# A selective-scan convolution with a gated FFN: another queue for one load, fewer idle products at the start, and the last group's products in another order

## The chip, the cores and the metric

The kernel runs on one core of a Trainium2 chip. Five engines work side by side, each through its own list of instructions: TensorE (PE, with its weight loads as PEld), VectorE (DVE), ScalarE (ACT), GpSimd (POOL) and SyncE (SP), which here only issues transfers. Semaphores order them. The metric is the device time of one execution in microseconds (us); lower is better.

## The reference, cut to what matters

```
# cond: a long convolution per head, K from the state space's poles
dtA = (-exp(log_A_real) + 1j*A_imag) * exp(log_dt)[:, None]
Ct  = (C[...,0] + 1j*C[...,1]) * (exp(dtA) - 1) / A
K   = 2 * einsum('hn,hnl->hl', Ct, exp(dtA[:,:,None] * arange(512))).real     # 32 heads x 512
y   = causal_conv(x, K) + x * D[:, None]                                      # 128 x 32 x 512
y   = y * (arange(512) < itok[:, None])[:, None, :]
# ffn along the length, each input rounded to fp8 (e4m3) with its scale
g = fp8(y) @ gate_w.T ; u = fp8(y) @ up_w.T                                   # 512 -> 1376
h = silu(g * scale) * (u * scale)
out = x + (fp8(h) @ down_w.T) * scale                                         # 1376 -> 512
```

There are 128 sequences (the batch), 32 heads and a length of 512. The FFN runs along the length, so that each pair of batch and head is one row of it, 4096 rows in all.

## The kernel before, in words

The length lies on the partitions in four chunks of 128, and a group is four heads times 128 sequences, 512 columns, so there are eight groups (g = 0 to 7).

**K and the convolution.** K is made on the chip in three batches of heads: heads 0 to 3, 4 to 15 and 16 to 31 (`batches`, L155). For a batch, `Powers` computes angles, magnitudes, sines and coefficients on VectorE and ScalarE, and `response` (L337) multiplies them on PE into `kp`, copies that to `kt` on VectorE and writes it to DRAM (`kpad`, L346). For a head, `toeplitz` (L435) reads 128 shifted rows of `kpad` back with two DMAs (L441, L442), which gives a Toeplitz matrix `st`. PE convolves with it in fp32 (`convolve` for the first two batches, `convolve8` with fewer products for the third, with `sp` and `cp` as accumulators). `conv` (L553) adds the shared part on VectorE, rounds to fp8 (`q`, L558) and masks it (L568).

**The first 30 us.** SyncE issues the loads in program order: the state space's planes `sm`, the scales (a broadcast of 3 KB), the lengths (a broadcast of 64 KB), group 0's input (1 MB, L121), and six of the eleven chunks of the gate matrix (1.5 MB, L146). Then come K's write and the Toeplitz reads of the first heads. ScalarE's first work is a table load, `sa` (L218) and the square `a2` (L220); then it waits for the step sizes. [...]`keep_busy` (L231) puts products of a zero tile (`nothing`) into its list: 14, then 12 behind `wim`, then 8 behind `th` (L356), then K's products of the first batch, then 22 more (L374).

**A group.** `gate_up` (L593) makes the 11 chunks of the hidden layer. For each, four products of `gw` into `gp` and four of `uw` into `up`; ScalarE takes silu (L612), VectorE multiplies (L613) into `v`, and two chunks at a time are rounded to fp8's grid by ScalarE (L586) and three VectorE operations (L589 to L591) into `hq`. Chunks 9 and 10 are rounded one by one, last. The batches of chunks are 0, 1-2, 3-4, 5-6, 7-8, 9, 10.

`Down` then multiplies `hq` by the down matrix, one tile `dp` of 128 rows of the length at a time, 11 products each (`multiply`, L644); `put_out` (L658) adds the result to `x` on VectorE (L662) and issues the output's DMA. While VectorE is still rounding, PE convolves the first two heads of the next group and starts tiles 0 and 1 without the two last chunks (`LATE` = 9, L634). Then it alternates: head 2, the rest of tile 0, head 3, the rest of tile 1, and at last tiles 2 and 3. Most groups have two accumulators for four `dp` tiles, so that tile 2 begins when tile 0 has been put out. In group 6 PE does only five products of tile 2 (`SOME`, L751) before the last gate/up; the other six and tile 3 follow behind it. Group 7's last tile is done in two halves of 256 columns.

**The order.** Each engine works through its list in order. The lists come from a planner that places instructions by its own estimate of when they are ready, within the order that `after(...)` prescribes. An accumulator or buffer is taken from a pool by its tag and is free when its last reader is done.

**The end.** `verdict` (L530) collects checks of the numbers on VectorE; one product `bp` (L542) sums them over partitions; the flag `any_bad` is read by every engine (L857), which then branches over a second, wider version of the kernel (L858).

Of the kernel before, what the change touches and what calls it, by code (L numbers as in the profile page):

```python
# [57 lines left out]
def ssm_fp8_ffn(  # L58
# [11 lines left out]
    nc = tc.nc  # L70
# [4 lines left out]
    IC = (I + P - 1) // P  # L75
    IP = IC * P
    NA, NB = 16, 32
    HG = 4
# [53 lines left out]
    gw = const.tile([P, LC, IP], F32, name="gw")  # L132
# [4 lines left out]
    def load_gate_up(w, src, i0, i1, queue=nc.sync):  # L137
        return queue.dma_start(w[:, :, i0:i1], src[:, i0:i1].rearrange("(c p) i -> p c i", p=P))
# [4 lines left out]
            nc.sync.dma_start(dw[0 : I - FI * P, FI, :], downT[FI * P :, :])  # L143

    IH = 6 * P
    load_gate_up(gw, gateT, 0, IH)  # L146

# [4 lines left out]
    batches = [(0, HG), (HG, HB), (HB, H)]  # L155
# [4 lines left out]
    EIGHT = len(batches) - 1  # L160
# [43 lines left out]
    def after(done):  # L204

        return tc.issue_after(done.ins)
# [11 lines left out]
    signs_there = nc.scalar.activation(sa, ca, AF.Copy, scale=sign)  # L218
    with after(signs_there):
        square_there = nc.scalar.activation(a2, aim, AF.Square)  # L220
    nc.gpsimd.tensor_mul(U, cb, aim)
    parts_there = nc.gpsimd.tensor_mul(V, sa, aim)
    ex = small("ex", [P, 2, H])
# [7 lines left out]
    def keep_busy(n, there=None):  # L231

        nothing = ps.tile([P, 512], F32, name="nothing", tag="gp")
        if there is not None:
            nc.tensor.matmul(nothing[0:NA, 0:NB], idx[:, 0:NA], there, start=True, stop=True)
        for _ in range(n):
            nc.tensor.matmul(nothing, still[:, 0:P], still, start=True, stop=True)  # L237
# [113 lines left out]
    th = small("th")  # L351
    with after(exp_there), after(square_there):
        silu_there = first.magnitudes()
    with after(silu_there):
        first_sines = first.sines(lambda: nc.scalar.activation(th, wre, AF.Tanh, scale=0.5))
    keep_busy(8, th)  # L356


    with after(parts_there):
# [12 lines left out]
    done, copied, _ = first.response()  # L372
# [38 lines left out]
    with after(build_mask(mask, all_bits, range(1))):  # L411
# [4 lines left out]
        done = build_mask(mask, all_bits, range(1, LC))  # L416
# [53 lines left out]
    def convolve(h, st, xg, xs, j, scale, pool, before=None, bufs=2):  # L470

        if h >= batches[EIGHT][0]:
            return convolve8(st, xg, xs, j, scale, pool, before, bufs)
        b = slice(j * B, (j + 1) * B)
        k3, k2, K2, K1, K0 = (st[:, n, :] for n in range(1, 6))
        sp = ps.tile([P, B], F32, name="sp", tag="gp")  # L480
        nc.tensor.matmul(sp, K2, xs[:, 0, b], start=True, stop=True)  # L481
        t = shared[j]
        with after(before) if before else ExitStack():
            copied = nc.scalar.activation(t[:, 1, :], sp, AF.Copy, scale=scale)
        cp = ps.tile([P, LC, B], F32, name="cp")
        nc.tensor.matmul(cp, K0, xg[:, :, b], start=True, stop=False)  # L486

        nc.tensor.matmul(cp[:, 2:4, :], K1, xg[:, 0:2, b], start=False, stop=False)  # L488
        nc.tensor.matmul(cp[:, 1, :], k2, xg[:, 2, b], start=False, stop=False)
        done = nc.tensor.matmul(cp[:, 3, :], k3, xg[:, 0, b], start=False, stop=True)  # L490
        return cp, twice(t[:, 0:2, :]), done, copied
# [53 lines left out]
    def narrow():  # L545
        with ExitStack() as arm:
# [3 lines left out]
            vp = arm.enter_context(tc.tile_pool(name="vp", bufs=3))  # L550
            gm, um, dm = (w.bitcast(BF16)[:, :, 1::2] for w in (gw, uw, dw))

            def conv(g, q, j, xg, xs, before, behind=None):  # L553

                st, loaded = toeplitz(stp, g * HG + j)
                cp, t, convolved, copied = convolve(g * HG + j, st, xg, xs, j, inv[:, 0:1], vp, before)
                with after(behind) if behind else ExitStack():
                    nc.vector.scalar_tensor_tensor(  # L558
                        pairs(q[:, :, j * B : (j + 1) * B]),
                        pairs(cp),  # L560
                        inv[:, 0:1],
                        t,
                        ALU.mult,
                        ALU.add,
                        saturate=False,
                    )
                words = q.bitcast(I32)[:, :, j * B // 4 : (j + 1) * B // 4]
                made = nc.vector.tensor_tensor(words, words, mask.bitcast(I32), ALU.bitwise_and)  # L568
                if j == HG - 1:
                    for n in range(2):  # L570
                        junk = vp.tile([P, T], F32, name="s")
                        nc.scalar.activation(  # L572
                            junk.bitcast(BF16),
                            q[:, n * LC // 2 : (n + 1) * LC // 2, :].rearrange("p c t -> p (c t)"),
                            AF.Abs,
                            accum_out=fin[:, 2 * g + n : 2 * g + n + 1],
                        )
                return convolved, made, loaded, copied
# [55 lines left out]
            LATE = IC - 2  # L634
# [45 lines left out]
            xg, xs = x0, xs0  # L680
# [23 lines left out]
            for g in range(G):  # L704
                sum_next = []
                hq, multiplied, sums, quantised = gate_up(
                    g, q, (lambda: sum_next.append(add_chunks(x_next, 1))) if g == 0 else lambda: None
                )
                if g == 2:
                    others[1].response()  # L710
                if g == G - 1:
                    break
                some = {0: (others[1].angles(), 2), 1: (itertools.chain(others[1].coefficients(), others[1].products()), 5)}
                tags = ["dp", "dp", "dp", "cp" if g == G - 2 else "dp"]
                d = Down(g, hq, xg, whole, tags, *some.get(g, ()))
                xg = x_next
                xs = sum_next.pop() if sum_next else xs
                q = yp.tile([P, LC, T], F8, name="q")

                def head(j, before):  # L720
                    return conv(g + 1, q, j, xg, xs, before)

                with after(multiplied):
                    head(0, sums[-2])
                    done, made, loaded, _ = head(1, sums[-1])
                if g == 0:
                    with after(loaded):
                        load_down()  # L730
                with after(sums[-1]):
                    if g == 0:
                        silu_there = others[1].magnitudes()
                    else:
                        list(itertools.islice(lows, 4))
                with after(done):
                    d.multiply(0, 0, LATE)
                    done = d.multiply(1, 0, LATE)
                for n in range(2):
                    with after(done):  # L740
                        done, made, loaded, _ = head(2 + n, sums[-1])
                    with after(done):
                        done = d.multiply(n, LATE, IC)
                    with after(made):
                        added = d.put_out(n)
                if g + 2 < G:
                    with after(loaded):
                        x_next = load_x(g + 2)
                        if (g + 2) * HG >= batches[EIGHT][0]:
                            xs = load_sums(g + 2)  # L750
                SOME = IC // 2  # L751
                with after(done):
                    done = d.multiply(2, 0, SOME)
                if g == G - 2:
                    continue
                with after(done):
                    done = d.multiply(2, SOME, IC)
                with after(added):
                    added = d.put_out(2)
                with after(done):  # L760
                    d.multiply(3, 0, IC)
                with after(added):
                    added = d.put_out(3)
                if g == 0:
                    with after(silu_there):
                        others[1].sines()
                if (g + 2) * HG < batches[EIGHT][0]:
                    with after(added):
                        xs = add_chunks(x_next, 1)

            with after(multiplied):
                d.multiply(2, SOME, IC)
                done = d.multiply(3, 0, IC)
            with after(quantised):
                d.put_out(2)
                added = d.put_out(3)
            d = Down(g, hq, xg, halves, ["dp", "gp", "up", "gp", "up"])
            with after(done):
                d.multiply(0, 0, LATE)
                done = d.multiply(1, 0, LATE)  # L780
            for n in range(len(halves)):
                with after(done):
                    done = d.multiply(n, LATE if n < 2 else 0, IC)
                    if n == len(halves) - 2:
                        with after(added):
                            verdict(done)
                d.put_out(n)
# [118 lines left out]
```

## Time and profile before

| | |
|---|---|
| median of 3 runs | 319.92 us (319.6 to 320.04) |
| the profiled execution's own time | 320.19 us |
| its span, first to last instruction | 318.4 us |
| PE busy | 308.7 us, 97% of the span |
| VectorE busy | 267.6 us, 84% |
| ScalarE busy | 182.4 us, 57% |
| GpSimd busy | 26.2 us, 8% |
| mean granted TensorE clock | 0.997 |
| DMA | 43.77 MB, 137 GB/s in the mean |

The profiled execution's time holds the span and some 1.8 us around it. Busy is what the profile's records cover; a matmul's record is longer than the time after which the next one may start, so that busy PE can hide small gaps, which show in the distance of starts only. In the timeline a row is the start, the time to the end of the last of its instructions, the engine, the line and operation, the tile written and those read, and the number of instructions. In the chain of work that ended last, a row is start, length and what it was.

### The profile page before, as it was taken

To read this page: it belongs to the slowest core of one execution; us is meant where nothing else is said; L and a number is where in the kernel's file an instruction comes from. 1 tells how busy PE (TensorE), PEld (TensorE's weight loads), DVE (VectorE), ACT (ScalarE), POOL (GpSimd) and SP (SyncE) were. 2 spreads that over 40 slices of the span, in tenths; PEclk is the share of its full clock that TensorE was granted. 3 is DMA by queue.
4 is the path that set the end of the run, shared out by engine and by line. 5 is a ranking of instruction groups with operands and counts; after the bars stand their busy time and mean duration, and the time that the engine had idled before them with its cause. 6 is when DMAs were issued, how large, how long until landed. Compare 5 with 4: busy or idle time off the path is not lost.

```text
span 318.4 us, 4632 instructions
## 1 busy us (share of the span) xinstructions
PE 308.7 (97%) x1583; PEld 165.4 (52%) x1583; DVE 267.6 (84%) x480; ACT 182.4 (57%) x372; POOL 26.2 (8%) x66
## 2 busy tenths in 40 slices
PE   8989999999999999999999999999999999999992
PEld 3455446544554446644576446644576446644441
DVE  5874999799989999648997699958997699969991
ACT  5825758567673668356673567456664576267600
POOL 5720000000000000120002200120001200000000
PEclk9999999999999999999999999999999999999998
DMA  3699999442036400698036921498046900010022
GB/s 95 260 234 382 264 357 309 129 134 89 12 86 193 141 1 2 132 312 228 1 99 194 280 90 48 110 286 219 2 99 171 256 4 2 1 66 3 0 106 102
DMA packets 32722, 43.77 MB, mean 137 GB/s; under 512 B 3539, under 2 KB 18899, under 8 KB 32691
## 3 DMA queue, kind: packets, MB, share of 16 engines
q1 hardware_dynamic: 29075, 34.61, 35.1%
q0 software_dynamic: 2560, 6.29, 9.2%
q10 hardware_dynamic: 1056, 2.49, 2.1%
q8 instruction: 14, 0.23, 0.3%
q14 instruction: 17, 0.14, 0.1%
HBM read 34.84 MB, written 8.55 MB: 136 GB/s over the span
## 4 chain that ended last, share of the span: by engine, by line
PE 78%; DVE 11%; ACT 3%; DMA 2%; issue 2%; POOL 1%; DVEq 0%; POOLq 0%; ACTq 0%
PE gp L604 22%; PE up L604 21%; PE dp L649 20%; PE cp L486 3%; PE sp L455 3%; PE cp L467 3%; DVE v L589 2%; DVE hq L590 2%; PE cp L465 2%; DVE v L613 2%; DVE q L558 2%; PE cp L488 2%; ACT mag L273 1%; PE sp L481 1%; DMA st<-kpad 1%
## 5 line engine op out<-in xcount | busy, mean ns | idle before, releaser
L604 PE MATMUL gp<-q,gw 128*128 128x512 fp8e4 x352 | 90.5, 379 | 0.7 <-DVE q L568 0.7
L604 PE MATMUL up<-q,uw 128*128 128x512 fp8e4 x352 | 90.3, 379 | 0.5 <-DVE v L613 0.5
L612 ACT ACTIVATE s<-gp,psc 128x512 f32<-128x512 f32 x88 | 59.9, 681 | 48.2 <-PE gp L604 48.1
L649 PE MATMUL dp<-hq,dw 128*128 128x512 bf16 (+1 forms) x363 | 80.6, 372 | 0.2
L613 DVE SCALAR_TENSOR_TENSOR v<-up,psc,s 128x512 f32<-128x512 f32 x88 | 65.4, 744 | 13.8 <-PE up L604 9.0
L589 DVE SCALAR_TENSOR_TENSOR v<-m,v 128x1024 f32<-128x1024 bf16 (+1 forms) x56 | 55.3, 988 | 5.4 <-ACT m L586 4.5
L586 ACT ACTIVATE m<-v 128x1024 bf16<-128x1024 f32 (+1 forms) x56 | 48.8, 872 | 17.4 <-DVE v L613 16.8
L604 PEld LDWEIGHTS <-uw 128*128 128x128 bf16 x352 | 34.5, 98 | 42.2 <-issue 0.8
L604 PEld LDWEIGHTS <-gw 128*128 128x128 bf16 x352 | 34.3, 98 | 42.4 <-issue 1.0
L590 DVE SCALAR_TENSOR_TENSOR hq<-m,v 128x1024 bf16<-128x1024 bf16 (+1 forms) x56 | 55.1, 984 | 0.1
L649 PEld LDWEIGHTS <-dw 128*128 128x128 bf16 x363 | 35.4, 98 | 37.1 <-issue 1.8
L662 DVE SCALAR_TENSOR_TENSOR xg<-dp,nsc,xg 128x512 f32<-128x512 f32 (+1 forms) x33 | 23.9, 731 | 10.8 <-PE dp L649 10.8
L558 DVE SCALAR_TENSOR_TENSOR q<-cp,inv,shared 128x512 fp8e4<-128x512 f32 x32 | 23.8, 745 | 9.6 <-PE cp L490 7.0
L572 ACT ACTIVATE s<-q 128x1024 bf16<-128x1024 fp8e4 x16 | 16.8, 1048 | 20.9 <-DVE q L568 20.9
L591 DVE TENSOR_SCALAR hq<-hq 128x1024 bf16<-128x1024 bf16 (+1 forms) x56 | 20.1, 358 | 0.2
L113 POOL DMA_DIRECT2D xs<-xT x4 | 3.2, 809 | 197.5 <-DVE q L558 114.6
L459 ACT ACTIVATE sh<-sp,inv 128x384 f32<-128x384 f32 x16 | 9.1, 571 | 15.9 <-PE sp L455 15.9
L237 PE MATMUL nothing<-still 128*128 128x512 bf16 x56 | 15.1, 430 | 1.4 <-POOL still L174 1.4
L486 PE MATMUL cp<-xg,st 128*128 128x512 f32 x32 | 16.4, 594 | 0.0
L455 PEld LDWEIGHTS sp<-xs,st 128*128 128x128 f32 x96 | 12.9, 192 | 1.7
L467 PEld LDWEIGHTS cp<-xg,st 128*128 128x128 f32 x96 | 13.2, 191 | 0.8
L455 PE MATMUL sp<-xs,st 128*128 128x128 f32 x96 | 13.3, 275 | 0.0
(143 smaller groups left out, 240.7 us busy)
## 6 DMA issues: line engine op xcount, KB each, us to landing
st<-kpad SPq DMA_DIRECT2D x48, 192.0 KB, 3.7
xg<-xT SPq DMA_DIRECT2D x8, 1024.0 KB, 6.6
outT<-xg SPq DMA_DIRECT2D x31, 256.0 KB, 4.7
xs<-xT POOLq DMA_DIRECT2D x8, 512.0 KB, 6.8
dw<-downT SPq DMA_DIRECT2D x1, 2560.0 KB, 13.3
st<-kpad SPq DMA_DIRECT2D x16, 128.0 KB, 4.3
xs<-xT POOLq DMA_DIRECT2D x8, 256.0 KB, 5.4
gw<-gateT SPq DMA_DIRECT2D x1, 1536.0 KB, 12.1
```

Of the source, the lines that this page charges most:

```text
L455: nc.tensor.matmul(sp[:, n, :], k, xs[:, n, b], start=True, stop=True)
L467: done = nc.tensor.matmul(cp[:, AT[c], :], k, xg[:, AT[x], b], start=c != 3, stop=True)
L486: nc.tensor.matmul(cp, K0, xg[:, :, b], start=True, stop=False)
L558: nc.vector.scalar_tensor_tensor(pairs(q[:, :, j * B : (j + 1) * B]), pairs(cp), inv[:, 0:1], t, ALU.mult, ALU.add, saturate=False,)
L586: done = nc.scalar.activation(m[:, 0:F], v, AF.Abs, scale=2.0**20 * (1.0 + 2.0**-6), accum_out=acc)
L589: nc.vector.scalar_tensor_tensor(v, m[:, 0:F], 1.5 * 2.0**14, v, ALU.max, ALU.add)
L590: nc.vector.scalar_tensor_tensor(out, m[:, 0:F], 1.5 * 2.0**14, v, ALU.max, ALU.subtract)
L604: multiplied = nc.tensor.matmul(o, w[:, c, i * P : (i + 1) * P], q[:, AT[c], :], start=(c == 0), stop=(c == LC - 1),)
L612: nc.scalar.activation(s, gp, AF.Silu, scale=pgate)
L613: product = nc.vector.scalar_tensor_tensor(v[:, (i - i0) * T : (i - i0 + 1) * T], up, pup, s, ALU.mult, ALU.mult)
L649: done = nc.tensor.matmul(self.dps[n], dm[:, i, c * P : (c + 1) * P], self.hq[:, i, t0:t1], start=(i == 0), stop=(i == IC - 1),)
L662: added = nc.vector.scalar_tensor_tensor(o, self.dps[n], ndown, o, ALU.mult, ALU.add)
```

## The change

Four edits.

1. The load of the first six gate chunks leaves SyncE's list, where it stood behind the input's load, and goes to ScalarE's, behind the square.
2. Eight zero products in front of the first batch's K become four.
3. In groups whose next group belongs to the third batch of heads (g = 3 to 6), the rest of tile 0 and its `put_out` come ahead of the VectorE operation that rounds head 2's convolution to `q`. PE's order stays.
4. Group 6 does all of tile 2, with its output, before the last gate/up. Group 7 starts three tiles without the last two chunks instead of two.

```diff
     IH = 6 * P
-    load_gate_up(gw, gateT, 0, IH)
...
     with after(signs_there):
         square_there = nc.scalar.activation(a2, aim, AF.Square)
+
+    with after(square_there):
+        load_gate_up(gw, gateT, 0, IH, nc.scalar)
...
-    keep_busy(8, th)
+    keep_busy(4, th)
...
-            def conv(g, q, j, xg, xs, before, behind=None):
+            def conv(g, q, j, xg, xs, before, behind=None, between=None):
                 st, loaded = toeplitz(stp, g * HG + j)
                 cp, t, convolved, copied = convolve(g * HG + j, st, xg, xs, j, inv[:, 0:1], vp, before)
+                if between:
+                    behind = between(convolved)
...
+                def finish(n, done):
+                    with after(done):
+                        return d.multiply(n, LATE, IC)
...
-                for n in range(2):
-                    with after(done):
-                        done, made, loaded, _ = head(2 + n, sums[-1])
-                    with after(done):
-                        done = d.multiply(n, LATE, IC)
-                    with after(made):
-                        added = d.put_out(n)
+                if (g + 1) * HG < batches[EIGHT][0]:
+                    for n in range(2):
+                        with after(done):
+                            done, made, loaded, _ = head(2 + n, sums[-1])
+                        done = finish(n, done)
+                        with after(made):
+                            added = d.put_out(n)
+                else:
+                    ends = []
+                    def first_out(convolved):
+                        ends.append(finish(0, convolved))
+                        return d.put_out(0)
+                    with after(done):
+                        head(2, sums[-1], first_out)
+                    with after(ends[0]):
+                        done, made, loaded, _ = head(3, sums[-1])
+                    done = finish(1, done)
+                    with after(made):
+                        added = d.put_out(1)
...
-                SOME = IC // 2
                 with after(done):
-                    done = d.multiply(2, 0, SOME)
+                    done = d.multiply(2, 0, IC)
+                with after(added):
+                    added = d.put_out(2)
                 if g == G - 2:
                     continue
-                with after(done):
-                    done = d.multiply(2, SOME, IC)
-                with after(added):
-                    added = d.put_out(2)
...
             with after(multiplied):
-                d.multiply(2, SOME, IC)
                 done = d.multiply(3, 0, IC)
             with after(quantised):
-                d.put_out(2)
                 added = d.put_out(3)
             d = Down(g, hq, xg, halves, ["dp", "gp", "up", "gp", "up"])
-            with after(done):
-                d.multiply(0, 0, LATE)
-                done = d.multiply(1, 0, LATE)
+            for n in range(3):
+                with after(done):
+                    done = d.multiply(n, 0, LATE)
             for n in range(len(halves)):
                 with after(done):
-                    done = d.multiply(n, LATE if n < 2 else 0, IC)
+                    done = d.multiply(n, LATE if n < 3 else 0, IC)
```

More of the change, by code (lines that the diff above doesn't have):

```diff
@@ L718, in narrow, with head @@
                 q = yp.tile([P, LC, T], F8, name="q")
-                def head(j, before):
-                    return conv(g + 1, q, j, xg, xs, before)
+                def head(j, before, between=None):
+                    return conv(g + 1, q, j, xg, xs, before, between=between)
+                def finish(n, done):
+                    with after(done):
+                        return d.multiply(n, LATE, IC)
                 with after(multiplied):
```

## The prediction

> **What bounds the kernel now.** The page comes first: PE is busy 97% of the span and the chain that ended last is 78% PE, so time comes only from stretches where PE has nothing useful to do: the start, two spots per group, and what follows the last matmul. The chain in order of time gives the start:
>
> ```profile
> 10.70 0.23 DVE ga L330
> ...
> 12.67 2.22 DMA kpad<-kt
> 14.89 0.02 issue
> 14.90 3.05 DMA st<-kpad
> 17.95 0.14 issue
> 18.09 0.46 PE sp L481 x2
> ```
>
> K goes out to DRAM and comes back as Toeplitz tiles before the first convolution at 18.09. The timeline shows what stands before it:
>
> ```profile
> 2.61 0.51 SPq L138 DMA_DIRECT2D gw<-gateT  x1
> ...
> 9.84 1.90 PE L237 MATMUL nothing<-still 128*128 128x512 bf16 x8
> ...
> 11.67 0.44 PE L341 MATMUL kp<-ang,ga 128*32 128x32 f32 x8
> ```
>
> `ga` is ready at 10.70 + 0.23 = 10.93, but K's matmuls start at 11.67, behind eight zero products. And K's write, issued at 12.67, follows gate's load on SyncE's queue. By windows of 1 us (last two columns: share of the DMA engines, GB/s):
>
> ```profile
> 11.00:12.00 1.00, 1.00 (x12) 0.46 (x10) 0.42 (x6) 1.00 (x6) 0.67 (x1) 1.00 0.99 399
> 12.00:13.00 1.00, 1.00 (x10) 0.54 (x7) 0.70 (x2) 1.00 (x6) 0.94 (x4) 1.00 0.54 214
> 13.00:14.00 1.00, 1.00 (x7) 0.46 (x5) 0.97 (x3) 0.98 (x2) 0.90 (x2) 1.00 0.54 191
> 14.00:15.00 1.00, 1.00 (x6) 0.42 (x5) 0.96 (x2) 0.70 (x2) 1.00 (x2) 1.00 0.05 12
> ```
>
> About half of the engines carry gate until 14; K's 18 KB land at 14.89, just after. Then the timeline of the groups whose next heads are of the third batch (g = 3 to 6), here g = 6:
>
> ```profile
> 277.39 0.75 DVE L662 SCALAR_TENSOR_TENSOR xg<-dp,nsc,xg 128x512 f32<-128x512 f32 x1
> 277.56 1.88 PE L649 MATMUL dp<-hq,dw 128*128 128x512 bf16 x7
> ...
> 279.94 1.02 PE L604 MATMUL gp<-q,gw 128*128 128x512 fp8e4 x4 [0.50 <-DVE q L568]
> ```
>
> Undisturbed down products start every 0.2157 us (four take 0.86 in the chain) and the last one shows 0.38; seven would take 6 x 0.2157 + 0.38 = 1.67, not 1.88. The missing 0.20 is tile 2 waiting for the accumulator that the first output frees at 278.14. Afterwards PE waits for the fourth head's q. At the end:
>
> ```profile
> 298.93 12.15 PE L649 MATMUL dp<-hq,dw 128*128 128x512 bf16 x61
> ...
> 303.30 0.42 DVE L591 TENSOR_SCALAR hq<-hq 128x1024 bf16<-128x1024 bf16 x1
> ```
>
> PE runs without a gap, but chunks 7 and 8 of hq come only at 303.72. Behind the last matmul stands SyncE (by line: duration min/median/max, first and last start; then its queue's waits):
>
> ```profile
> L857 SPq TENSOR_LOAD <-any_bad x1: 488/488/488, 312.0 to 312.0; - x1
> L665 SPq DMA_DIRECT2D outT<-xg x7: 332/332/333, 306.7 to 313.1; - x7
> L858 SPq COMPARE_BRANCH  x1: 45/45/45, 313.4 to 313.4; - x1
> L858 SPq EVENT_SEMAPHORE  x8: 17/17/17, 316.2 to 316.7; - x8
> SPq L858 <- SPq L858: 2.7, 1, 2.7
> ```
>
> SyncE reads the flag at 312.0, issues the last output at 313.1, branches at 313.4, comes to life 2.7 us later, and its row of semaphore waits runs to the end at 318.4.
>
> **What the skill says.** "TensorE: Matmul & The Clock Gate", on why a gap is 56 ns and not 53.3, gives 215.7 ns from start to start for 512 columns on a warm array; this trace has 0.86/4 = 0.2157, the price used below. The same page, on the clock gate, lets PE cool after some 3.4 us of idling; here PE idles 0.95 us before the first convolution and stays at clock 1.00. "DMA: Bandwidth & Descriptors", Queues, rings and completion order: each issuing engine has its own ring on every DMA engine, a ring is drained in order, and rings take turns. The windows above agree with the first half (K's write ends with gate's load); two full rings side by side are not shown by any run yet. The same page, Issuing engines are not separate DMA queues: another queue adds no bandwidth. So the total of input (1 MB) and gate (1.5 MB) takes as long as before once it runs.
>
> **The change, part by part.**
>
> *Four zero products fewer.* 4 x 0.2157 = 0.86 would let K start at 10.81; `ga` at 10.93 plus some 0.05 (as q to gp, 27.36 to 27.41) holds it to 10.98. Gain 0.69. VectorE's small work ends at 11.45, before it must copy K (12.30 - 0.69 = 11.61). The 22 products that follow cover PE as before.
>
> *Gate's first load on ScalarE's queue.* ScalarE issues it at 3.32, after the square; two such issues took 0.42 and 0.71 there, and ScalarE then waits 2.4 us for its exponentials in any case: cost nothing, 0.4 to 0.7 without that cover. On SyncE it passes nothing that waits. The transfer: at 3-5 us the engines are 3 to 4% busy (2 and 13 GB/s), the input, as I read it, stuck behind the two small broadcasts on its ring. I expect gate to fill this from about 4.3 (some 1 us from issue to data: after the read issued at 14.90 the engines are at 0.04 until 16 and at 0.68 from then) and both, 2.5 MB at some 400 GB/s = 6.3 us, to be in by about 11 on all engines. The input then lands later than its 2.14 + 8.7 = 10.84, near 11.5, still ahead of the add of its chunks (12.51 - 0.6). The lengths, landing at 8, have 2.1 us of GpSimd's wait before the masks as cover. K's write then finds empty rings. The third batch's write, 88 KB alone on the engines, took about 2.0 from issue to reading back (SyncE's three waits on such writes are 9.9 with one of 6.4 and the first 1.8, plus 0.33 to issue); with a fifth of the rows about 1.58. Against 2.22 this is a gain of 0.64; bounds: none, if gate is still running, and 0.8. SyncE's later issues all follow K's landing, and DMA is nearly full from 16 to 55 us on work that starts with it, so all of it shifts along. Start: -1.33; PE's 22 products cap the start's gain at 18.09 - 16.45 = 1.64.
>
> *First output ahead of the third head's q.* As built, VectorE's order in g = 3 to 6 is: shared part, output 0, q of head 2, shared part of head 3, mask, q of head 3. The same work, with the mask no longer waiting directly behind its q. Output 0's product is complete at 275.95, when VectorE is still on the shared part, so nothing waits. Output 0 then ends near 277.0, and tile 2 starts without waiting: by the same reading (four in 1.16, 1.22, 1.23 where 1.03 is due, seven in 1.88) 0.13 + 0.19 + 0.20 + 0.20 = 0.72. Tile 3 needs output 1, at g = 5 ready 0.1 before its turn and now some 0.3 earlier: no new wait.
>
> *Tile 2 of g = 6 whole before the last gate/up; three tiles without two chunks.* PE's work is unchanged: six down products move from behind the last gate/up to before it. They hide the wait for q: before, 7 x 0.2157 + 0.20 after 277.56 is 279.27, and gp starts at 279.94: 0.67 gone. Now gp starts at 277.56 + 13 x 0.2157 = 280.37. But at the other end these six covered VectorE. hq 7 and 8 are ready 303.72 - 279.94 = 23.78 after gate/up starts, a time set by VectorE's own work (in the group before also 23.78: 270.76 - 246.98). Before, PE reaches chunk 7 at 298.93 + 24 x 0.2157 = 304.11, 0.39 late enough. Now it has 11 + 7 products first: 18.99 + 18 x 0.2157 = 22.87 after the start, so it stands 23.83 - 22.87 = 0.96 in the first of the three tiles. Beginning the third tile adds cover only for chunks 9 and 10, which had enough. Output 2 of g = 6 goes into VectorE's idle 1.5 us before the first v. Sum: -0.67 + 0.96 = +0.29.
>
> *Not named in the words of the change:* as built, SyncE issues both last outputs before it reads the flag. From the read's start at 312.02 through register work to the next wait at 312.88 it spent 0.86, then hidden in its wait for the last output; now this stands between the last issue and the branch. Price 0.86; bounds 0 (if another engine's branch ends last; they come to life at 314.9 to 316.5) and 0.9.
>
> Sum: -1.33 - 0.72 + 0.29 + 0.86 = -0.90. Against the profiled execution's 320.19 (span 318.4 and 1.8 around it) this is 319.3; against the median of 319.92, which lies 0.27 lower, 319.0.
>
> **Rivals.** (B) One of the two losses doesn't come: SyncE's branch is not last, or VectorE quantises sooner. 319.0 - 0.9 = 318.1. For it: the other engines come to life within 0.3 us of SyncE. Against: SyncE's own row of waits follows its branch, wherever that stands. (C) The new queue gains nothing, since gate starts no earlier than before and only the zero products count: 319.0 + 0.64 = 319.6. For it: late in the trace ScalarE's loads, issued at 20.6, land at 31.7. Against: the rings were full then. (D) Slower: gate still runs when K is written and read back, and now takes turns with it. Each engine carries 9 of K's rows and 8 of a Toeplitz tile's; if each of them waits for one 3 KB row of gate (3072 x 16 / 400 GB/s = 0.12 us), K's write takes 1.58 + 1.1 and the tile 3.05 + 1.0: the start is -0.69 + 0.45 + 1.0 = +0.8 in place of -1.33, or 321.1. It decides from gate's last row after about 13.5. Against: the estimate of 11.
>
> **How the numbers follow.** The forecast 0.52, its own range 318.5 to 319.5; B 0.22; C 0.18; D 0.08. Two per mille, 0.64 us, is about what tells a change from none, so faster means under 319.28: 0.8 of the forecast and all of B, 0.64. C and the rest of the forecast make 0.28 the same, D 0.08 slower. The range 317.9 to 320.0 takes in B and C.
>
> **What would show it.** K's matmuls at 11.0 and not 11.7; K's write landing 1.5 to 1.7 after its issue; first convolution near 16.8; full-rate down products at tile 2 in g = 3 to 6; no wait before the last gate/up; a wait of about 1 us for hq in the down products after it; SyncE's read and branch after the last output's issue, its row of waits starting some 3.6 us after that issue and not 2.7+0.4. The prediction is wrong if DMA is still busy with gate at 12 to 14, or if the last stretch has no wait.

## The result, and the profile after

The changed kernel takes 320.45 us in the median (320.23 to 321.11, 17 runs) against 320.19 of the kernel before (319.6 to 321.28, 17 runs). The ratio is 1.0012 with a 95% interval of 1.0004 to 1.0020: slower by about a thousandth, where 319.0 was forecast. The profiled span grew from 318.4 to 318.9 us.

**The start** did not move. The timeline of the changed kernel (start, time to the end, engine, operation):

```profile
2.92 0.42 ACTq L138 DMA_DIRECT2D gw<-gateT  x1
...
11.16 0.44 PE L342 MATMUL kp<-ang,ga 128*32 128x32 f32 x8
...
12.15 0.38 SPq L347 DMA_DIRECT2D kpad<-kt  x1
14.90 0.35 SPq L442 DMA_DIRECT2D st<-kpad  x1
```

K's products start 0.5 earlier than before (11.16, not 11.67), and so does K's write (12.15, not 12.67). But the write is read back at 14.90, to the hundredth where it was, and the chain that ended last has the first convolution at 18.02, where it had 18.09. The windows of 1 us say why (the last two columns are the share of the DMA engines that is busy and GB/s):

```profile
3.00:4.00 1.00, 1.00 (x4) 0.41 (x3) 0.93 (x7) 0.31 (x2) 0.36 (x2) 1.00 0.05 8
4.00:5.00 1.00, 1.00 (x4) 0.34 (x3) 0.86 (x5) 0.00 (x0) 0.00 (x0) 1.00 0.05 16
...
12.00:13.00 1.00, 0.95 (x6) 0.41 (x6) 1.00 (x3) 1.00 (x6) 0.94 (x4) 1.00 0.55 211
13.00:14.00 1.00, 1.00 (x5) 0.47 (x5) 0.97 (x3) 0.98 (x2) 0.90 (x2) 1.00 0.48 168
14.00:15.00 1.00, 1.00 (x7) 0.46 (x5) 0.97 (x3) 0.69 (x2) 1.00 (x2) 1.00 0.04 11
```

From 3 to 5 the engines still stand at 5%: the load that ScalarE issued at 2.92 does not run in the idle time that the forecast gave it. The records of the transfers, told apart by queue and packet size, have gate's first row at 7.86 (before: 8.04) and its last at 14.24 in both kernels. K's write again meets it at 12 to 14: its rows run in bursts, none of them starts between 13.79 and 14.24, while gate's last ten begin, and its last twelve start from 14.24 to 14.34, right behind the end of gate's.

The records allow a closer look. On every engine that it uses, a transfer closes with a record of 4 bytes: sixteen for the input and for gate, twelve for K's write. Each of the input's sixteen closing records is followed within 6 ns by a row of gate. Eight engines are through with gate at 12.1, and K's first 96 rows run from 12.96 to 13.12, beside gate's rows on the other eight. The remaining 48 come in four bursts of twelve, at 13.20, 13.55, 13.69 and 14.24, and each burst starts within 0.01 of a closing record of gate (13.20, 13.54, 13.68, 14.23). The records don't name the engine, but by these times each engine does all of the input before gate, and all of gate before K's rows, although gate is on another queue.

**Tile 2 of g = 6**, in PE's timeline:

```profile
277.10 2.97 PE L652 MATMUL dp<-hq,dw 128*128 128x512 bf16 x12
279.91 1.03 PE L607 MATMUL gp<-q,gw 128*128 128x512 fp8e4 x4
```

Thirteen products, one of them missing from the records, take 12 x 0.2157 + 0.38 = 2.97: full rate, and gate/up follows with no idle time noted. The waits at tile 2 in g = 3 to 5 are gone too.

**The last stretch:**

```profile
299.12 3.83 PE L652 MATMUL dp<-hq,dw 128*128 128x512 bf16 x17
...
303.26 0.43 DVE L594 TENSOR_SCALAR hq<-hq 128x1024 bf16<-128x1024 bf16 x1
...
303.75 1.02 PE L652 MATMUL dp<-hq,dw 128*128 128x512 bf16 x4 [0.80 <-DVE hq L594]
```

The last of the 17 products starts at 299.12 + 3.83 - 0.38 = 302.57, and the next at 303.75, when VectorE has chunks 7 and 8: 1.18 from start to start, less 0.216, is a new wait of 0.97. Last, SyncE by line (duration in ns, first and last start in us):

```profile
L874 SPq TENSOR_LOAD <-any_bad x1: 491/491/491, 313.1 to 313.1; - x1
L668 SPq DMA_DIRECT2D outT<-xg x33: 332/337/1055, 59.8 to 312.7; - x33
L875 SPq COMPARE_BRANCH  x1: 45/45/45, 313.9 to 313.9; - x1
L875 SPq EVENT_SEMAPHORE  x8: 17/17/17, 316.7 to 317.3; - x8
```

The flag is read at 313.1, now behind the last output's issue at 312.7. From the end of VectorE's last output, 312.19 + 0.48 = 312.67, to the first semaphore at 316.72 it is 4.05; before it was 3.15.

### The profile page after: what moved, and what is told of

It reads as the page before. It is cut to its first block, busy times and chain, and to the rows that moved or that the text cites. A ratio compares the mean times of both kernels' runs of the same rounds, so it can differ in the third digit from the quotient of the medians.

```text
span 318.9 us, 4604 instructions
## 1 busy us (share of the span) xinstructions
PE 306.8 (96%) x1563; PEld 165.2 (52%) x1579; DVE 266.8 (84%) x480; ACT 182.6 (57%) x372; POOL 25.7 (8%) x66
## 4 chain that ended last, share of the span: by engine, by line
PE 84%; DVE 10%; ACT 2%; issue 1%; POOL 0%; DVEq 0%; POOLq 0%
PE gp L607 22%; PE up L607 21%; PE dp L652 20%; PE sp L456 3%; PE cp L468 3%; PE cp L487 3%; PE nothing L238 3%; PE cp L466 2%; DVE v L592 2%; DVE v L616 2%; PE cp L489 2%; DVE hq L593 2%; ACT mag L274 1%; PE sp L482 1%; PE cp L491 1%
## 5 line engine op out<-in xcount | busy, mean ns | idle before, releaser
L652 PE MATMUL dp<-hq,dw 128*128 128x512 bf16 (+1 forms) x348 | 78.1, 372 | 1.7 <-DVE hq L594 0.8
```

The lines of the kernel that those rows point to most:

```text
L652: done = nc.tensor.matmul(self.dps[n], dm[:, i, c * P : (c + 1) * P], self.hq[:, i, t0:t1], start=(i == 0), stop=(i == IC - 1),)
```

## The experiments

My theory after the result: a transfer engine serves the two queues in the order of issue, so gate cannot pass the broadcasts and the input wherever it is issued from, and K's write cannot be read back before gate is through. Everything else happened as forecast, with two losses (the wait for hq, SyncE's end) as large as the two gains. The rival for the start: the queue, the table load ahead of gate's load, or something else at 14.9 that has nothing to do with gate. The theory held for gate and for K's write; as a rule for all transfers it did not, as the kernel with gate first shows. For the end: the two losses may hide behind one another. No kernel here leaves any computation out.

### Gate's load back on SyncE's queue

```diff
     IH = 6 * P
+    load_gate_up(gw, gateT, 0, IH)
...
-    with after(square_there):
-        load_gate_up(gw, gateT, 0, IH, nc.scalar)
```

> The changed kernel with the gate load back on SyncE's queue, behind the input. Theory 'order of issue' (each DMA engine works through rows in the order in which the transfers were issued, whichever queue they came from): K's write lands at 14.9 as with ScalarE's queue, the time stays within 0.2 of the changed kernel's 320.45. Theory 'own queue helps a little' (the rings take turns, only gate's start was late): K's write lands some 0.3 later and the time rises by as much, to 320.75.

320.47 us against 320.11, ratio 1.0006 (0.9993 to 1.0019). Gate's rows run from 7.83 to 14.21, K's write takes from 11.96 to 14.86, the first convolution is at 18.02, the wait for hq is 0.97. The queue makes no difference that can be measured, in the time or at any of these places.

### The broadcasts taken away

The host hands the scales and the lengths over as 128 equal rows, so that each partition reads a row of its own; bytes, queue and place in the list stay.

```diff
-    nc.sync.dma_start(sc, scales.to_broadcast([P, 6]))
+    nc.sync.dma_start(sc, scales)
...
-    nc.sync.dma_start(len_i, lens.to_broadcast([P, B]))
+    nc.sync.dma_start(len_i, lens)
```

> The changed kernel, but lengths and scales are handed over as 128 equal rows in DRAM, so that the two broadcasts no longer read one row 128 times; same work otherwise. Theory 'broadcasts first': they hold the engines with 8 slow rows each, so the input starts at 5.3 and gate ends at 14.2; without them the input starts near 3, gate is in by 11, K's write of 12.0 lands after some 1.6 in place of 2.7, the first convolution starts near 16.9 instead of 18.0 and the time is 320.45 - 1.1 = 319.3. Rival 'K's landing has its own length' (the write's receipt, not the queue in front of it): the input may start sooner, but the write takes 2.2 to 2.7 again and the time stays at 320.45.

319.50 us, ratio 0.9973 (0.9959 to 0.9987). The timeline:

```profile
10.99 0.44 PE L342 MATMUL kp<-ang,ga 128*32 128x32 f32 x8 [0.33 <-DVE ga L331]
...
11.99 0.38 SPq L347 DMA_DIRECT2D kpad<-kt  x1
13.40 0.35 SPq L442 DMA_DIRECT2D st<-kpad  x1
```

The input's rows begin at 3.27 instead of 5.15, gate's end at 11.28, and K's write is read back 1.41 after its issue, not 2.75. K's products at 10.99 and the write at 11.99 are the forecast's own numbers (10.98, and 12.67 - 0.69 = 11.98), and 1.41 is better than its 1.58. Not all of it arrives: the first Toeplitz read takes 3.57 here, where it takes 2.9 to 3.4 in the other eleven traces, so the first convolution is at 17.10. Why this one read is slower I did not find out. The first gate/up is at 26.42 instead of 27.43.

The same with eight zero products again:

```diff
-    keep_busy(4, th)
+    keep_busy(8, th)
```

> The same with eight zero products in front of K again. If the fewer zero products are worth something once DMA is out of the way: K's products start some 0.4 to 0.7 later than with four, and so does everything after, 319.7 to 320.0. If something else still sets the first convolution: as with four, 319.3.

319.90 us, ratio 0.9989 (0.9976 to 1.0003). Its write is issued at 12.52, its first convolution is at 17.01 and its first gate/up at 26.33. The medians lie 0.4 apart in favour of four products, the intervals overlap, and the two traces show no difference after the Toeplitz read.

### Gate first of all

```diff
     IH = 6 * P
+    load_gate_up(gw, gateT, 0, IH, nc.scalar)
...
-    with after(square_there):
-        load_gate_up(gw, gateT, 0, IH, nc.scalar)
```

The load keeps ScalarE's queue, but is now issued at 0.75, before the scales (1.20), the lengths (1.68) and the input (2.14) on SyncE's.

> The changed kernel with the gate load as the first of all on ScalarE's queue, ahead of its table load, so that it is issued before SyncE's broadcasts and input. Theory 'order of issue': gate's rows run from 1.7 to 5.7 while nothing else is wanted, the broadcasts and the input follow, all is in by 11 and K's write lands after 1.6: 319.3; the state space's planes may come 0.3 later than 2.8, which would give 319.6. Theory 'rings take turns': gate also starts early, but the broadcasts and the input share with it; the same end. If gate starts at 7.5 again, ScalarE's queue itself is late and neither holds.

319.47 us, ratio 0.9976 (0.9963 to 0.9990). The windows of this kernel:

```profile
4.00:5.00 1.00, 1.00 (x4) 0.34 (x3) 0.86 (x5) 0.00 (x0) 0.00 (x0) 1.00 1.04 415
5.00:6.00 1.00, 1.00 (x3) 0.29 (x2) 0.84 (x5) 0.11 (x1) 0.35 (x2) 1.00 0.99 373
6.00:7.00 1.00, 1.00 (x4) 0.29 (x2) 0.88 (x3) 0.98 (x5) 1.00 (x4) 1.00 0.65 204
...
12.00:13.00 1.00, 1.00 (x5) 0.46 (x5) 0.66 (x2) 1.00 (x6) 0.94 (x4) 1.00 0.04 12
13.00:14.00 1.00, 0.95 (x5) 0.42 (x5) 0.97 (x3) 0.98 (x3) 0.90 (x2) 1.00 0.12 18
```

and its timeline:

```profile
12.31 0.38 SPq L346 DMA_DIRECT2D kpad<-kt  x1
13.72 0.35 SPq L441 DMA_DIRECT2D st<-kpad  x1
```

The engines, idle from 4 to 5 in the other kernels, now move 415 GB/s. Gate's rows run from 2.08 to 7.92. The scales, 3 KB on the other queue, were issued at 1.20; their first row starts at 5.31 (2.25 in the changed kernel), and the input's rows follow from 8.22 to 12.17. So a short transfer with nothing unfinished before it on its own queue but the 96 KB of the planes, which start at 1.78 and end by 2.7, begins 4 us after its issue, behind some 300 of the 512 rows of the long one on the other queue.

But it doesn't wait for the end of gate. By 5.31 no engine can be through with its 32 rows of gate, which take 0.12 each from 2.08 on, and gate's first closing record comes at 7.56. From 5.31 on the rows of the two queues alternate: 124 of the scales' 128 rows are followed by a row of gate within 8 ns (by chance it would be some 60), and the scales have closed on all sixteen engines by 7.49, before gate has on any. From 6 to 7 the engines move only 204 GB/s. Here the two queues do take turns, row by row; input and gate, or gate and K's write, did not in the changed kernel. What decides between the two I did not find out.

K's write at 12.31 finds the engines at 4% and takes 1.41. The first gate/up is at 26.10. With the runs without broadcasts this settles the start: what holds K's write back is gate's transfer, and what holds gate back is the broadcasts and the input, issued before it.

### The changed kernel with eight zero products

The edit is that of the second pair above, alone.

> The changed kernel with eight zero products in front of K instead of four, edit 2 alone undone. If K's write waits on every transfer engine for gate's rows, K's products start some 0.45 later, the write is issued near 12.6 instead of 12.15, and it is read back at 14.9 as before: first convolution within 0.1 of 18.0, time within 0.3 of the changed kernel's (320.1 to 320.7). If the earlier write does count, the first convolution comes near 18.45 and the time is 0.4 to 0.5 longer than the changed kernel's.

320.79 us against 320.04, ratio 1.0023 (1.0012 to 1.0033). Its trace doesn't show what it was made for: in the profiled execution PE was ahead with its zero products, so that K's products started at 11.04, earlier than with four, and the write at 12.04 was still read back at 14.61 only. Its last twelve rows start at 13.94, again right behind a closing record of gate (13.94); the first convolution is at 17.80. The time is some 0.35 above the changed kernel's, with intervals that overlap; the median spans, 318.7 and 318.6, lie 0.1 apart. The chain of the kernel with edit 3 alone, which has eight zero products and gate on SyncE's queue like the kernel before, shows the same more plainly:

```profile
11.98 2.63 DMA kpad<-kt
14.62 3.37 DMA st<-kpad
```

There K's products happen to start at 10.98 and the write is issued at 11.98, just as edit 2 was to bring about, and the first convolution is at 18.12 all the same. Together with the pair above it leaves open whether four products fewer are worth up to 0.4; edits 1 and 2 together are worth nothing, as the next two runs show.

### Edit 3 alone, and all but edit 4

The first kernel is the kernel before with the branch on `(g + 1) * HG < batches[EIGHT][0]` and the `between` argument; the second is the changed kernel with edit 4 undone:

```diff
+                SOME = IC // 2
                 with after(done):
-                    done = d.multiply(2, 0, IC)
-                with after(added):
-                    added = d.put_out(2)
+                    done = d.multiply(2, 0, SOME)
...
-            for n in range(3):
+            for n in range(2):
...
-                    done = d.multiply(n, LATE if n < 3 else 0, IC)
+                    done = d.multiply(n, LATE if n < 2 else 0, IC)
```

> The kernel before with the third edit alone (first output ahead of the third head's q in groups 3 to 6). Theory: the four waits of tile 2 go, 0.13 + 0.19 + 0.20 + 0.20 = 0.72, and the wait for q before the last gate/up falls by up to 0.3 as VectorE works without pauses: 0.7 to 1.0 under the kernel before, 319.2 to 319.5. Rival: the waits only move to tile 3 or to the next group's q, 320.2.

> The changed kernel without its fourth edit: five products of tile 2 before the last gate/up, six behind it, two tiles begun without two chunks; the planner's read of the flag is then ahead of the last output again. Theory: the fourth edit costs 0.97 - 0.67 = 0.3 for hq and 0.86 for the flag, so without it 320.45 - 1.16 = 319.3. Rival: the wait for hq would have come in any case, 319.6 or more.

Edit 3 alone: 319.06 us against 320.05, ratio 0.9971 (0.9960 to 0.9982). Without edit 4: 319.14, ratio 0.9969 (0.9956 to 0.9981). So edit 3 is worth about 1.0, edits 1 and 2 add nothing to it, and edit 4 turns 319.1 into the changed kernel's 320.4. PE in the kernel without edit 4:

```profile
276.95 1.67 PE L652 MATMUL dp<-hq,dw 128*128 128x512 bf16 x7
278.82 1.02 PE L607 MATMUL gp<-q,gw 128*128 128x512 fp8e4 x4 [0.19 <-DVE q L571]
```

Seven products take the full-rate 1.67 (1.88 before), and the wait for q behind them is 278.82 - 276.95 - 7 x 0.2157 = 0.36, where it was 0.67. Edit 3 alone took away 0.3 of the wait that the forecast gave to edit 4. VectorE shows how. Before:

```profile
275.68 0.55 DVE L463 TENSOR_TENSOR shared<-sh 128x384 f32<-128x384 f32 x1
276.33 0.75 DVE L558 SCALAR_TENSOR_TENSOR q<-cp,inv,shared 128x512 fp8e4<-128x512 f32 x1
277.12 0.29 DVE L568 TENSOR_TENSOR q<-q,mask 128x128 int32<-128x128 int32 x1
...
278.06 0.55 DVE L463 TENSOR_TENSOR shared<-sh 128x384 f32<-128x384 f32 x1
278.72 0.75 DVE L558 SCALAR_TENSOR_TENSOR q<-cp,inv,shared 128x512 fp8e4<-128x512 f32 x1
279.50 0.29 DVE L568 TENSOR_TENSOR q<-q,mask 128x128 int32<-128x128 int32 x1
```

With edit 3 alone:

```profile
275.22 0.55 DVE L463 TENSOR_TENSOR shared<-sh 128x384 f32<-128x384 f32 x1
275.69 0.75 DVE L664 SCALAR_TENSOR_TENSOR xg<-dp,nsc,xg 128x512 f32<-128x512 f32 x1
276.35 0.74 DVE L560 SCALAR_TENSOR_TENSOR q<-cp,inv,shared 128x512 fp8e4<-128x512 f32 x1
277.07 0.56 DVE L463 TENSOR_TENSOR shared<-sh 128x384 f32<-128x384 f32 x1
277.55 0.28 DVE L570 TENSOR_TENSOR q<-q,mask 128x128 int32<-128x128 int32 x1
277.75 0.74 DVE L560 SCALAR_TENSOR_TENSOR q<-cp,inv,shared 128x512 fp8e4<-128x512 f32 x1
278.53 0.29 DVE L570 TENSOR_TENSOR q<-q,mask 128x128 int32<-128x128 int32 x1
```

Before, the left-out line is the first output, at 277.39. The same seven operations take 3.82 from the first start to the last before, and 3.31 with edit 3. Before, four of the six steps are to an operation that reads what the one in front has just written, and it starts 0.03 to 0.11 after that one's end (276.33 against 275.68 + 0.55). With edit 3 only the last step is of that kind; the others start 0.02 to 0.09 before the end of their forerunner. So the fourth head's q is ready half a microsecond earlier with no work removed.

### The three last tiles begun without four chunks

```diff
+            EARLY = LATE - 2
             for n in range(3):
                 with after(done):
-                    done = d.multiply(n, 0, LATE)
+                    done = d.multiply(n, 0, EARLY)
...
-                    done = d.multiply(n, LATE if n < 3 else 0, IC)
+                    done = d.multiply(n, EARLY if n < 3 else 0, IC)
```

As built, SyncE reads the flag ahead of the last output again.

> The changed kernel, with the three last tiles begun without four chunks instead of two, so that chunks 7 and 8 are wanted 21 products later at the earliest; by the planner this also puts the read of the flag ahead of the last output. Theory: the wait of 0.97 for hq in the last down products goes, and the 0.86 of the flag, 320.45 - 1.83 = 318.6. Rival: the wait only moves to chunks 9 and 10 or to the outputs, 319.6 (the flag alone).

318.83 us, ratio 0.9962 (0.9950 to 0.9975). PE's timeline from 299 on:

```profile
299.06 5.78 PE L652 MATMUL dp<-hq,dw 128*128 128x512 bf16 x26
```

26 products in 25 x 0.2157 + 0.38 = 5.77, without a wait. From the last output's end to SyncE's first semaphore it is 2.98. Against the changed kernel this is some 1.6 less; the two losses sum to 1.87, within what the intervals allow.

### The flag read ahead of the last output, alone

```diff
             for n in range(len(halves)):
                 with after(done):
                     done = d.multiply(n, LATE if n < 3 else 0, IC)
+                if n == len(halves) - 1:
+                    flag.append(nc.values_load(any_bad[0:1, 0:1], min_val=0, max_val=1))
...
-    bad = nc.values_load(any_bad[0:1, 0:1], min_val=0, max_val=1)
-    with tc.If(bad > 0):
+    with tc.If(flag[0] > 0):
```

> The changed kernel with only SyncE's order at the end altered: it reads the flag and works on its register before it waits for the last output, as in the kernel before. Theory 'read behind the last output costs 0.86': SyncE's branch comes 0.86 earlier after the last output and the span is shorter by that, 319.6. Rival 'another engine's branch ends last': no more than 0.3, 320.2.

320.11 us against 320.05, ratio 1.0005 (0.9994 to 1.0015, 14 runs between 319.49 and 321.14). In the trace the way from the last output to the first semaphore is 3.12, not 4.05, so the 0.9 is there in that execution. The medians show only some 0.2 of it. The spans explain the difference: in six of the 14 executions 2.3 to 2.5 us of the time lie outside the span, where it is some 1.8 to 1.9 in the other eight (of the changed kernel's 17 executions three have more than 2.2), and no profile shows what that is. The median span is 317.95, and the changed kernel's is 318.6: 0.65 for SyncE's order. The other kernels agree. From the end of the last output to SyncE's first semaphore it is 3.82 to 4.05, in the mean 3.89, in the traces of the six kernels that read the flag behind the last issue, and 2.95 to 3.31, in the mean 3.12, in the six that read it ahead: 0.77. By median spans, with the wait of 0.97 and the 0.36 taken at their measured size, going from the changed kernel to the one without edit 4 (318.6 to 317.2) leaves 0.8 for SyncE, and going to four chunks (318.6 to 316.9) leaves 0.7. So this order costs 0.65 to 0.8.

### Gate first and four chunks together

> The changed kernel with two edits at once: gate's first load is issued ahead of everything else on ScalarE's queue, and the three last tiles begin without four chunks instead of two. If what was measured of each adds up, the start gives 1.0 (first gate/up near 26.2 instead of 27.4), the end gives 0.97 (no wait for hq in the down products of the last stretch) and SyncE's flag read, back ahead of the last output, 0.9: a span near 316.0 and a median near 317.5 to 318.0 beside 320.1 of the kernel before. If the two losses of the end hide behind each other, as the step from the changed kernel to the one with four chunks suggests (1.6 where 0.97 + 0.9 was due), it is 317.8 to 318.2.

317.89 us against 320.04, ratio 0.9925 (0.9911 to 0.9939): faster than both kernels. The chain that ended last, at the start:

```profile
0.75 2.60 DMA sm<-ssm
...
12.64 1.50 DMA kpad<-kt
14.14 0.02 issue
14.16 2.97 DMA st<-kpad
17.13 0.14 issue
17.27 0.46 PE sp L481 x2
```

and K's products in its timeline:

```profile
11.64 0.44 PE L341 MATMUL kp<-ang,ga 128*32 128x32 f32 x8 [0.86 <-DVE ga L330]
```

and SyncE at the end:

```profile
L874 SPq TENSOR_LOAD <-any_bad x1: 630/630/630, 310.0 to 310.0; - x1
...
L667 SPq DMA_DIRECT2D outT<-xg x33: 332/337/1109, 59.1 to 311.0; - x33
```

Gate first has a price here. It is issued at the same moment as the planes `sm`, and they land 2.60 after their issue; in the chain of the kernel before the line is

```profile
0.75 2.04 DMA sm<-ssm
```

All of VectorE's work on K follows the planes: `ga` ends at 11.59 and not 10.92, and K's products wait for it until 11.64 (with gate first alone 11.32). So the first gate/up came at 26.77 only; the write still took 1.5, and the flag is read before the last output. The gains of the start and of the end add up: the median span is 316.0, 2.6 under the changed kernel's, where gate first and four chunks alone have 1.0 and 1.7.

## Why the prediction was wrong

The step that failed is **the transfer**: "I expect gate to fill this from about 4.3", and with it "both ... to be in by about 11" and "K's write then finds empty rings". The idle 3 to 5 us were read rightly as the input standing behind the two broadcasts, and wrong was the conclusion that a load on another queue could pass them. It began at 7.86, on each engine right behind the input's last row. The start gave +0.03 at the first gate/up (27.433 against 27.406) instead of -1.33; the first convolution had come 0.07 earlier (18.02 against 18.09). The sum, with that one term replaced, is +0.03 - 0.72 + 0.29 + 0.86 = +0.46; the span grew by 0.5 and the median by 0.26.

- **Four zero products fewer**, -0.69: K's products did start 0.5 earlier, and the write too, but a write that is read back only when gate is through turns this into a longer write (2.75 for 2.22). The forecast saw this dependence for the 0.64 of the write ("none, if gate is still running") and not for the 0.69 in front of it. The two gains had one condition and were priced as if they had two. The size was also read from one execution, in which it happened to be largest. In all twelve traces the first zero products start 0.43 apart and later ones 0.22 apart, and the change comes between 4.20 and 7.33. It came at 6.03 in the trace before; in the other three traces with eight zero products in front of K it came at 5.93, 4.75 and 4.23, and K's products started at 11.53, 11.04 and 10.98, where the forecast had 11.67 for eight and 10.98 for four.
- **The write with free engines**, 1.58 forecast, is 1.41 in the two runs that clear the engines; there the first gate/up comes 1.0 and 1.3 earlier. The mechanism and the size were right, and only the edit doesn't bring it about.
- **Edit 3**: the 0.72 of the tile-2 waits came as worked out. Missing was the half microsecond on VectorE, which shortens the wait before the last gate/up by 0.3. Alone it is worth 1.0.
- **Edit 4**: the sum +0.29 was right, as that wait is gone with both edits. The split was not: with edit 3 in place edit 4 removes 0.36 and not 0.67, so edit 4 is a loss of 0.6 before SyncE is counted. The new wait for hq was forecast as 0.96 and is 0.97.
- **SyncE's order**: forecast 0.86. It is 0.90 between the traces of the two kernels, 0.77 between the means of all twelve, and 0.65 by the median spans.
- **Rivals.** C had the cause ("gate starts no earlier than before"), but kept the zero products' gain; without it, it gives 319.6 + 0.69 = 320.3. D, that gate takes turns with K's write and its read-back, fell: K's rows wait and don't take turns, and the Toeplitz read took no longer than before. Its count of nine rows of K on each engine was off, too: the closing records show twelve engines, so twelve rows on each. PE's wait before the first convolution is 0.97 in the trace, not 0.95. B did not come.

The Trainium skill, "DMA: Bandwidth & Descriptors", Queues, rings and completion order, was drawn on for rings that take turns. The traces show it for one pair of transfers and not for others. Gate waits for the input when it is issued after it, and K's rows wait for gate's last row, each time across two queues and without a turn; with gate first, the scales come late but then alternate with gate's rows from 5.31 to 7.49. The same section says that SyncE's and ScalarE's queues have no descriptor generator of their own. A shared generator that works through the issues in order would give the scales' late start; it doesn't by itself say why K's rows took no turns. No run looked into it, and where the order arises is open.

## What to carry to other kernels

Don't count on a second queue to bring a load forward past what was issued before it: here it did nothing for gate. Issue the load earlier, or take away the slow transfers in front of it, and look at what it then delays (with gate first, the planes). Before a gain is priced from one execution, look whether other executions show the same size. When several gains rest on one condition, price them together, for both cases of the condition. When products are moved from one end of a group to the other, look at which wait they covered where they stood, and look at how the instructions fall on every queue, SyncE's last ones included.

## What the runs showed that I had not expected

- Transfers on different queues began in the order of issue: 3 KB of scales, issued 0.45 after 1.5 MB of gate on another queue, began 4.1 after their issue. Then they alternated with gate row by row and were through before it; gate behind the input, and K's write behind gate, took no turns at all.
- Reading the same row of memory into 128 partitions is slow. The scales (3 KB) and the lengths (64 KB) as broadcasts held the input back until 5.15; as 128 rows of their own, with the same bytes, the input began at 3.27.
- Order alone changes VectorE's time: an operation that reads the result of the one just in front started 0.03 to 0.11 after its end, an independent one 0.02 to 0.09 before it. Six such steps made 0.51.
- How long PE's zero products take at the start differs between executions, as the change of their distance from 0.43 to 0.22 comes at 4.20 in one and at 7.33 in another. Behind eight of them K's products started at 10.98 to 11.67. Behind four they started at 11.16 in the changed kernel, and in the seven other traces they waited for `ga` and not for PE. One execution can hide a difference of this size.
